# Zero fill of a row buffer moved from GpSimd's queue to SyncE's, with context rows loaded earlier into three buffers

## The chip, the cores and the metric

The kernel runs on one core of a Trainium2 chip, in one launch. The metric is the device time of that launch in microseconds (us): the median over the runs of the program. Five engines of the core take part, each working through its own list of instructions in order: TensorE (PE) multiplies matrices and transposes, VectorE (DVE) and ScalarE (ACT) do elementwise work and reductions, GpSimd (POOL) does the same more slowly and issues indirect transfers, and SyncE (SP) issues most of the plain transfers (DMAs). Engines wait for each other, and for DMAs, on semaphores. All data are float32.

## The reference

A stream `x` of 16 sequences of 128 tokens with 256 channels passes four layers. Each layer is a cross attention to a context `ctx` (16 x 128 x 256), followed by a feed-forward part; both are added to `x` with the weight tanh of a gate. Cut to the first layer, where the change lies:

```python
x = x + tanh(g_xattn[0]) * L0_xattn(ctx, layernorm(x), ctx, Wk, Wq, Wv, Wo)   # 16 heads of 16
x = x + tanh(g_ffn[0])   * L0_ffn(layernorm(x), w_gate, W1, b1, W2, b2)       # 8 experts, the best 2

def L0_xattn(k, q, v, Wk, Wq, Wv, Wo):          # k = v = ctx
    kh, qh, vh = per_head(k, Wk), per_head(q, Wq), per_head(v, Wv)
    attn = softmax(qh kh^T / sqrt(16))
    return concat_heads(attn vh) @ Wo.T

def L0_ffn(x, w_gate, W1, b1, W2, b2):
    gate = softmax(x @ w_gate.T); pick the two largest experts of every token
    return sum over the two of gate_e * (gelu(x @ W1[e] + b1[e]) @ W2[e] + b2[e])
```

The other three layers have the same frame, with other attentions (softmax over queries, a key mask, latents beside the context) and other feed-forward parts (low rank adapters, two more mixtures of experts).

## The kernel before

**Tiling.** The 2048 tokens stand as 16 tiles of 128 tokens, one for each sequence (`b`), and four tiles make a block (`blk`, `BPB` = 4, `NBLK` = 4). For attention layer 0 the class `Fast16` folds the weights of queries and keys into one matrix and those of values and output into another, so keys and values come straight from the context: the keys from its transpose `ctxT` (one tile for each block, loaded through ACT's queue), the values from its rows `ctx_rows` (one tile of 512 KB for each block, loaded through SP's queue).

**Steps of a sequence.** `scores(b)` copies the context rows of `b` into the padded value tile (ACT, L1288), multiplies keys by queries (PE, L1301) and takes the exponential (ACT, L1316). `values(b)` multiplies the exponentials by values and by ones (PE, L1357), takes the reciprocal of the sums into `rs` (DVE, L1368), adds `rs` into a running sum `sum_range` on POOL (L1126; it is looked at once, at the end of the program) and multiplies (DVE, L1370). `output(b)` multiplies by the folded output matrix (PE, L1379) and adds to `x` (DVE, L363). `rs` has two buffers, so the third reciprocal in a row can only start once POOL has read the first.

**Order.** `attend` writes the order of PE, DVE and ACT by hand: it interleaves the steps of 16 sequences with the preparation of the next block (layer norm of `x` with ACT L321 writing `xn`, transposes with PE L344, query projection) and, three steps after a block's last sequence, with the "front" of the mixture of experts of that block (`Moe.front`: a layer norm, the router, positions of the tokens, and the scatter). POOL and SP are not in that hand-written order; a scheduler places their instructions by their dependencies.

**The row buffer.** The mixture of experts sorts tokens by expert: each front writes the normalized rows of its block into a buffer in device memory, `xg` (17,280 rows of 260 numbers, 18 MB), with eight indirect DMAs issued by POOL (L558). Rows that no token takes must be zero, so `xg` is filled with zeros before the first scatter. That is the job of `clear` (L2445 on), a generator that runs ahead of a block's layer norm: for block 1 it makes a tile `zeros` on POOL (L2452) and issues 15 DMAs of 1170 KB on POOL's queue (L2458). For block 2 it issues the first guess of expert weights `w` on SP's queue (L1653), with small bias tiles `b` (L1660, L1667). After the front of block 1 the positions are known, SP reads the plan and fetches rows `xr` and weights, and the expert matmuls (L1701) begin while attention goes on.

**Buffers and queues that the change touches.** `ctx_rows` has two buffers and is loaded by `Fast16.load_rows`: block 0 when the object is made, block `blk + 1` when block `blk` is prepared. `xn` has three buffers, shared by all layer norms. At most eight DMAs of SP and ACT together are in flight: in the built program each waits on a counter for the completion of the one eight before it. POOL's DMAs have eight such counters of their own.

Of the kernel before, what the change touches and what calls it, by code (L numbers as in the profile page):

```python
# [8 lines left out]
F32 = mybir.dt.float32  # L9
# [10 lines left out]
P = 128  # L20
B = 16
S = 128
D = 256
KC = D // P
NBLK = 4
BPB = B // NBLK
TB = BPB * S
# [18 lines left out]
ROWS = NE * REGION + (NE - 1) * P  # L46
# [3 lines left out]
ROW = D + 4  # L50
# [40 lines left out]
def kernel(ctx: ExitStack, tc: tile.TileContext, a: dict, out: bass.AP):  # L91
    nc = tc.nc
# [3 lines left out]
    stat = ctx.enter_context(tc.tile_pool(name="stat", bufs=2))  # L96
    rpool = ctx.enter_context(tc.tile_pool(name="route", bufs=2))
    xtpool = ctx.enter_context(tc.tile_pool(name="xnT", bufs=NBLK))
    class Ring:


        def __init__(self, pool):
            self.pool, self.made = pool, []
# [15 lines left out]
    def load_x(bs):  # L119
        for b in bs:  # L120
            nc.sync.dma_start(out=xs[b], in_=a["x"][b * S:(b + 1) * S, :])
# [9 lines left out]
        out=gates, in_=a["rows"][:, slice(*_ROWS["gates"])].to_broadcast([P, 8])  # L131
# [4 lines left out]
    def col(name, i):  # L136
        lo = _COLS[name][0] + i
        return cols[:, lo:lo + 1]
# [18 lines left out]
    for e in range(NE):  # L157
# [9 lines left out]
        out=tri, in_=ones, compare_op=ALU.is_gt, fill=0.0, base=0,  # L167
# [27 lines left out]
    def tgx(i):  # L195
        return tg[:, i:i + 1]

    def gate_down(pool, i):

        gate = pool.tile([P, 1], F32, tag=f"gate{i}", name="gate", bufs=1)  # L200
        nc.vector.tensor_scalar(gate, tgx(i), DOWN, None, ALU.mult)
        return gate
# [959 lines left out]
    def keys_in(pool):  # L1162
        return lambda: pool.tile([P, KC, TB], F32, tag="kT", name="kT", bufs=2)

    class Fast16:

        def __init__(
            self, layer, pool, kpool, w, ctxT, watch, mask=None, bias=None, others=None  # L1170
        ):

            self.others = others
            self.bias = bias
            self.gate = tgx(1) if layer == 1 else gate_down(pool, layer)
            self.layer, self.pool, self.kpool = layer, pool, kpool
            self.ctxT, self.watch, self.mask = ctxT, watch, mask
            self.w = w

            self.qb = pool.tile([P, KC, 2], F32, tag=f"qb{layer}", name="qb", bufs=1)  # L1180
            if layer == 0:
                nc.vector.memset(self.qb, 0.0)
            else:
                for c in range(KC):
                    nc.vector.tensor_scalar(
                        self.qb[:, c, :], mask2, col(f"l{layer}_bq", c), None, ALU.mult
                    )

            self.vs = []
            for i in range(3):  # L1190
                v = pool.tile([P, H16, 2 * DH16], F32, tag=f"v{layer}{i}", name="v", bufs=1)
                nc.gpsimd.memset(v, 0.0)
                self.vs.append(v)
            self.qM, self.kT, self.es, self.os = {}, {}, {}, {}
            self.rows = {}
            if layer == 0:
                self.kT = dict(enumerate(ctxT))
                self.load_rows(0)

        def load_rows(self, blk):  # L1200

            t = self.pool.tile([P, BPB, D], F32, tag="crows", name="ctx_rows")
            nc.sync.dma_start(
                out=t,
                in_=a["ctx"][blk * TB:(blk + 1) * TB, :].rearrange("(b p) d -> p b d", p=P),
            )
            self.rows[blk] = t

        def prepare(self, blk, before):


            if self.layer == 0 and blk + 1 < NBLK:
                self.load_rows(blk + 1)
            made = [self.queries(blk, before)]
            if blk not in self.kT:
                made.append(self.keys(blk))
            if self.others is not None:

                if blk == 0:
                    made.append(self.keys(1))  # L1220
                for later in (0, 1, 2) if blk == 0 else (3,) if blk == 1 else ():
                    made.append(self.others.keys(later))
            return made
# [1147 lines left out]
    def layers(fast):  # L2371
# [40 lines left out]
        with tc.tile_pool(name="context", bufs=1) as cpool, ExitStack() as for_mid:  # L2412
            ctxT = []

            def load_context(blk):
                t = cpool.tile([P, KC, TB], F32, tag=f"ctxT{blk}", name="ctxT")
                nc.scalar.dma_start(
                    out=t,
                    in_=a["ctxT"][:, blk * TB:(blk + 1) * TB].rearrange("(k p) t -> p k t", p=P),
                )  # L2420
                ctxT.append(t)
# [7 lines left out]
            with tc.tile_pool(name="att0", bufs=2) as pool:  # L2429
                w = attention_weights(0, pool)  # L2430
                if fast:
                    load_x(range(BPB, 2 * BPB))
                load_context(1)
                if fast:
                    nc.sync.dma_start(out=cols, in_=a["cols"])
                    nc.sync.dma_start(out=rows, in_=a["rows"].to_broadcast([P, N_ROWS]))
                    wgs[0] = gate_weights("l0")
                if fast:
                    load_x(range(2 * BPB, B))
                for blk in range(2, NBLK):  # L2440
                    load_context(blk)
                if fast:
                    wgs[2], wgs[3] = gate_weights("l2"), gate_weights("l3")
                moe = Moe(0, wgs[0], first_turn)

                def clear(blk):
                    if blk == 1:


                        n = 9  # L2450
                        zeros = pool.tile([P, 1, 3 * ROW], F32, tag="zeros", name="zeros", bufs=1)
                        nc.gpsimd.tensor_scalar(  # L2452
                            zeros.rearrange("p o (r d) -> p (o r) d", d=ROW),
                            att.kT[0][:, 0:1, 0:ROW].to_broadcast([P, 3, ROW]),
                            0.0, 0.0, ALU.min, ALU.max,
                        )
                        for i in range(0, ROWS, n * P):
                            nc.gpsimd.dma_start(  # L2458
                                out=xg[i:i + n * P, :].rearrange(
                                    "(p r q) d -> p r (q d)", p=P, q=3  # L2460
                                ),
                                in_=zeros.to_broadcast([P, n // 3, 3 * ROW]),
                            )
                    if blk == 2 and fast:
                        moe.guess = {0: 0, 1: 3}
                        for get_some in first0, second0:
                            for lane, e in moe.guess.items():
                                tc.add_manual_dep(
                                    get_some(lanes[lane], e, None).ins, run["aggr"].name,
                                    mybir.DependencyInfo(  # L2470
                                        mybir.DependencyClass.Sync,
                                        mybir.DependencyReason.DATA,
                                    ),
                                    reason="behind the first loads",
                                )
                    if blk == NBLK - 1 and fast:
                        mask.extend(mask_by_keys(cpool, mi))
                    yield 1


                n = full_slots(NBLK // 2) if fast else 0
                turns = {NBLK - 1: cycle((2, 1, 0), NSLOT - n)}
                started = []

                def start(plan):
                    started.append(slots0(moe, n, [plan], lanes, tiles(fpool, bufs0)))

                def early():
                    while not started:
                        yield 1  # L2490
                    yield from started[0]

                if fast:
                    turns[NBLK // 2 - 1] = cycle((0, 1), n)
                    lanes = lane0(fpool, 2)
                else:
                    lanes = []
                behind, plans = routed(moe, turns, start)
                if fast:
                    att = Fast16(0, pool, None, folded(pool, w), ctxT, watch)  # L2500
                    attend([(att, clear, behind)], early(), eager=True, express=2)
                else:
                    general(shifted(pool, 0, w, ctxT), None, behind)
# [5 lines left out]
            with for_slots, tc.tile_pool(name="lanes0", bufs=2) as pool:  # L2509
                lanes = lanes + lane0(pool, LANES - len(lanes))  # L2510
                job = slots0(moe, NSLOT - n, plans[-1:], lanes, tiles(fpool, bufs0))
                for i, _ in enumerate(job):
                    if i == 24:
                        ws = [attention_weights(layer, wpool) for layer in (1, 2)]
                        if not biases:

                            t = stat.tile([P, BPB, ROW], F32, tag="xn", name="bias_rows", bufs=3)
                            nc.sync.dma_start(
                                out=t[:, 0, 0:D],
                                in_=a["l2_b2"][NE:NE + 1].to_broadcast([P, D]),  # L2520
# [60 lines left out]
        with ExitStack() as for_last:  # L2581
# [19 lines left out]
            turns, n = {}, 0  # L2601
# [136 lines left out]
```

## Time and profile before

| what | value |
|---|---|
| time, median of 3 runs | 1607.16 us (1603.55 to 1607.68) |
| profiled execution, its own time | 1651.63 us |
| span of its trace | 1649.8 us |
| PE busy | 1506.4 us (91%) |
| DVE, ACT, POOL busy | 867.0, 639.7, 368.5 us |
| DMA traffic | 173.61 MB, of it 15 transfers of 1170 KB from `zeros` to `xg` |

The profile is of one execution, on the only core. Times in it count from the start of its span. A row of the timeline gives start, duration, engine, line, operation and tiles, the number of instructions merged into it, and in brackets the idle time of the engine ahead of it with what ended that idle time. "SPq" and "POOLq" are the engines' own queues, where issuing a DMA stands. In a table of windows, "DMA share" is the busy share of the 16 DMA engines and "PEclk" the clock that TensorE was granted, as a part of full speed.

### The profile page before, as it was taken

To read this page: it belongs to the slowest core of one execution; us is meant where nothing else is said; L and a number is where in the kernel's file an instruction comes from. 1 tells how busy PE (TensorE), PEld (TensorE's weight loads), DVE (VectorE), ACT (ScalarE), POOL (GpSimd) and SP (SyncE) were. 2 spreads that over 40 slices of the span, in tenths; PEclk is the share of its full clock that TensorE was granted. 3 is DMA by queue.
4 is the path that set the end of the run, shared out by engine and by line. 5 is a ranking of instruction groups with operands and counts; after the bars stand their busy time and mean duration, and the time that the engine had idled before them with its cause. 6 is when DMAs were issued, how large, how long until landed. Compare 5 with 4: busy or idle time off the path is not lost.

```text
span 1649.8 us, 34723 instructions
## 1 busy us (share of the span) xinstructions
PE 1506.4 (91%) x12681; PEld 1178.4 (71%) x12681; DVE 867.0 (53%) x2766; ACT 639.7 (39%) x1538; POOL 368.5 (22%) x485
## 2 busy tenths in 40 slices
PE   5787899999989999999999999999999999888892
PEld 3565789999656567645559999999846665567792
DVE  4666312223289767656346555556734553557564
ACT  4554333335556566452225333334442324123010
POOL 4234211112533112433000111011150002203431
PEclk8897999999999999899999999999999999999896
DMA  9913574524420000111064414310260000024856
GB/s 314 384 60 125 190 244 137 186 85 152 100 33 1 1 14 15 41 40 52 0 220 151 152 42 139 119 33 28 98 122 1 14 5 24 24 85 137 261 175 206
DMA packets 111480, 173.61 MB, mean 105 GB/s; under 512 B 17337, under 2 KB 81406, under 8 KB 111296
## 3 DMA queue, kind: packets, MB, share of 16 engines
q1 hardware_dynamic: 87456, 116.32, 22.4%
q0 software_dynamic: 20304, 49.66, 9.7%
q10 hardware_dynamic: 3536, 5.25, 1.0%
q8 instruction: 107, 1.75, 0.5%
q14 instruction: 77, 0.63, 0.1%
HBM read 274.98 MB, written 48.18 MB: 196 GB/s over the span
## 4 chain that ended last, share of the span: by engine, by line


## 5 line engine op out<-in xcount | busy, mean ns | idle before, releaser
L1878 PEld LDWEIGHTS ps_w<-xT,w 128*128 128x128 f32 x2304 | 264.3, 192 | 2.6 <-issue 0.2
L1878 PE MATMUL ps_w<-xT,w 128*128 128x128 f32 x2304 | 265.0, 275 | 0.0
L878 POOL DMA_INDIRECT yd<-y,to x117 | 118.6, 1014 | 581.2 <-DVE c L841 318.8
L866 PE MATMUL ps_e<-w,hT 128*128 128x256 f32 x848 | 198.5, 380 | 4.1 <-DVE hT L1785 1.9
L866 PEld LDWEIGHTS ps_e<-w,hT 128*128 128x128 f32 x848 | 154.5, 190 | 24.0 <-DVE hT L1785 2.8
L1886 ACT ACTIVATE u<-ps_w,b 128x128 f32<-128x128 f32 x312 | 89.6, 367 | 174.7 <-PE ps_w L1878 165.7
L1889 DVE SCALAR_TENSOR_TENSOR m<-ps_w,b,u 128x128 f32<-128x128 f32 x312 | 87.6, 344 | 108.9 <-PE ps_w L1878 90.7
L1701 PE MATMUL ps_h<-xT,w 128*128 128x128 f32 x1120 | 135.0, 280 | 10.3 <-DMA w<-in_l_w_dram 5.4
L1701 PEld LDWEIGHTS ps_h<-xT,w 128*128 128x128 f32 x1120 | 133.3, 196 | 13.9 <-issue 6.9
L1706 ACT ACTIVATE hT<-ps_h,b 128x128 f32<-128x128 f32 x312 | 88.1, 371 | 134.9 <-issue 81.3
L558 POOL DMA_INDIRECT xg<-xn,xi x96 | 93.5, 974 | 103.9 <-issue 54.6
L1815 PE MATMUL ps_w<-xnT,sw 128*128 128x512 f32 x256 | 113.1, 598 | 0.0
L874 DVE SCALAR_TENSOR_TENSOR y<-ps_e,c,bias 128x256 f32<-128x256 f32 x78 | 37.6, 482 | 133.4 <-PE ps_e L866 132.6
L1126 POOL TENSOR_TENSOR sum_range<-sum_range,rs 128x256 f32<-128x256 f32 x48 | 35.3, 735 | 273.8 <-DVE rs L2295 144.2
L831 DVE COPY xT<-ps_xr 128x256 f32<-128x256 f32 x117 | 48.5, 418 | 84.1 <-PE ps_xr L829 71.1
L1815 PEld LDWEIGHTS ps_w<-xnT,sw 128*128 128x128 f32 x256 | 48.6, 192 | 57.9 <-issue 51.6
L1368 DVE RECIPROCAL rs<-ps_o 128x256 f32<-128x256 f32 x32 | 56.2, 1756 | 59.4 <-PE ps_o L1357 32.3
L1316 ACT ACTIVATE e<-ps_s 128x512 f32<-128x512 f32 x128 | 65.9, 602 | 36.2 <-PE ps_s L1301 33.1
L1357 PE MATMUL ps_o<-e,v 128*32 128x128 f32 x1536 | 58.5, 292 | 15.9 <-issue 4.8
L321 ACT ACTIVATE xn<-x,nmr,rstd 128x256 f32<-128x256 f32 x128 | 67.7, 597 | 13.1 <-DVE nmr L314 9.5
L1357 PEld LDWEIGHTS ps_o<-e,v 128*32 128x32 f32 x1536 | 43.0, 116 | 33.6 <-issue 16.6
L2274 ACT ACTIVATE e<-ps_s 128x512 f32<-128x512 f32 x64 | 33.8, 600 | 80.5 <-PE ps_s L2268 77.1
(280 smaller groups left out, 2566.2 us busy)
## 6 DMA issues: line engine op xcount, KB each, us to landing
w<-in_l_w_dram SPq DMA_DIRECT2D x160, 1024.0 KB
w<-in_l_w_dram SPq DMA_DIRECT2D x39, 512.0 KB
kT<-in_l_wgu_dram SPq DMA_DIRECT2D x39, 512.0 KB
xg<-zeros POOLq DMA_DIRECT2D x15, 1170.0 KB
b<-in_l_b_dram SPq DMA_DIRECT2D x80, 128.0 KB
xr<-xg SPq DMA_DIRECT2D x78, 130.0 KB
kT<-in_l_w_dram SPq DMA_DIRECT2D x39, 256.0 KB
x<-yd POOLq DMA_DIRECT2D x48, 128.0 KB
```

Of the source, the lines that this page charges most:

```text
L321: nc.scalar.activation(xns[:, i, 0:D], src, AF.Identity, bias=nmr[:, i:i + 1], scale=rstd[:, i:i + 1])
L558: self.unordered(nc.gpsimd.indirect_dma_start(out=xg[:, :], in_=xns[:, i, :], in_offset=None, out_offset=bass.IndirectOffsetOnAxis(ap=xi[: ...
L866: nc.tensor.matmul(po, lhsT=hT[:, f, :], rhs=lane(s)["w2"][:, f, :], start=(f == 0), stop=(f == nf - 1),)
L878: self.unordered(nc.gpsimd.indirect_dma_start(out=yd[:, :], in_=y, in_offset=None, out_offset=bass.IndirectOffsetOnAxis(ap=to[:, 0:1], axi ...
L1316: nc.scalar.activation(e, pss[j], AF.Exp)
L1357: nc.tensor.matmul(po[32 * j:32 * (j + 1), i, c, :], lhsT=w if i else v[:, c * HPC + 2 * j + e, :], rhs=es[j][:, 2 * c + e, :], start=(e = ...
L1701: nc.tensor.matmul(ps[:, i, :], lhsT=w["w1"][:, k, f * P:(f + 1) * P], rhs=xT[:, k, :], start=(k == 0), stop=(k == KC - 1),)
L1706: nc.scalar.activation(hT[:, f, :], ps[:, i, :], AF.Gelu, bias=w["b1"][:, f:f + 1])
L1815: nc.tensor.matmul(ps, lhsT=wt[:, k, f * P:(f + 1) * P], rhs=xnT[:, k, :], start=(k == 0), stop=(k == KC - 1),)
L1878: nc.tensor.matmul(ps[:, f, :], lhsT=wt[:, k, s, f * P:(f + 1) * P], rhs=xT[:, k, :], start=(k == 0), stop=(k == KC - 1),)
L1886: nc.scalar.activation(u[:, f, :], pair[0][:, f, :], AF.Identity, bias=w["b1"][:, i:i + 1])
L1889: nc.vector.scalar_tensor_tensor(m1[:, f, :], pair[1][:, f, :], w["b3"][:, i:i + 1], u[:, f, :], ALU.add, ALU.mult,)
```

## The change

The context rows are loaded by a function outside the class, into three buffers. Block 0's rows are loaded on SP's queue ahead of the second four tiles of `x`, block 1's right behind these; block 2's and 3's are loaded when blocks 1 and 2 are prepared. The tile `zeros` is no longer a tile of its own: it takes a buffer of the `xn` ring (three buffers), and it is made from block 1's context rows in place of the transposed context. The 15 zero DMAs are issued by SP: the first six when block 1 is prepared, behind the load of block 2's context rows, and nine more when block 2 is prepared, behind the load of block 3's.

```diff
+    ctx_rows = {}
+    def load_rows(pool, blk):
+        t = pool.tile([P, BPB, D], F32, tag="crows", name="ctx_rows", bufs=3)
+        nc.sync.dma_start(
+            out=t,
+            in_=a["ctx"][blk * TB:(blk + 1) * TB, :].rearrange("(b p) d -> p b d", p=P),
+        )
+        ctx_rows[blk] = t
...
-            self.rows = {}
+            self.rows = ctx_rows
             if layer == 0:
                 self.kT = dict(enumerate(ctxT))
-                self.load_rows(0)
...
-            if self.layer == 0 and blk + 1 < NBLK:
-                self.load_rows(blk + 1)
+            if self.layer == 0 and 1 <= blk < NBLK - 1:
+                load_rows(self.pool, blk + 1)
...
                 if fast:
+                    load_rows(pool, 0)
                     load_x(range(BPB, 2 * BPB))
                 load_context(1)
                 if fast:
+                    load_rows(pool, 1)
                     nc.sync.dma_start(out=cols, in_=a["cols"])
...
+                cleared = []
                 def clear(blk):
+                    n = 9
                     if blk == 1:
-                        n = 9
-                        zeros = pool.tile([P, 1, 3 * ROW], F32, tag="zeros", name="zeros", bufs=1)
+                        zeros = stat.tile([P, BPB, ROW], F32, tag="xn", name="zeros", bufs=3)
+                        zeros = zeros.rearrange("p b d -> p (b d)")[:, None, 0:3 * ROW]
                         nc.gpsimd.tensor_scalar(
                             zeros.rearrange("p o (r d) -> p (o r) d", d=ROW),
+                            ctx_rows[1].rearrange("p b d -> p (b d)")[:, 0:3 * ROW].rearrange(
+                                "p (r d) -> p r d", d=ROW
+                            ) if fast else
                             att.kT[0][:, 0:1, 0:ROW].to_broadcast([P, 3, ROW]),
                             0.0, 0.0, ALU.min, ALU.max,
                         )
-                        for i in range(0, ROWS, n * P):
-                            nc.gpsimd.dma_start(
+                        cleared.append(zeros)
+                    if blk in (1, 2):
+                        at = ROWS * 2 // 5
+                        for i in range(*((0, at) if blk == 1 else (at, ROWS)), n * P):
+                            nc.sync.dma_start(
                                 out=xg[i:i + n * P, :].rearrange(
                                     "(p r q) d -> p r (q d)", p=P, q=3
                                 ),
-                                in_=zeros.to_broadcast([P, n // 3, 3 * ROW]),
+                                in_=cleared[0].to_broadcast([P, n // 3, 3 * ROW]),
                             )
```

`ROWS` is 17,280, `P` 128 and `ROW` 260, so `n * P` is 1152 rows for each DMA and `at` is 6912 rows, six DMAs. In the built program the order of PE, DVE and ACT is the same before and after, instruction by instruction. On SP's queue it becomes: block 0's rows ahead of `x` tiles 4 to 7, block 1's behind them, the other early loads as before, then block 2's rows, six zero DMAs, block 3's rows, nine zero DMAs, then the first guess of expert weights and biases.

More of the change, by code (lines that the diff above doesn't have):

```diff
@@ L1194, in __init__ @@
             self.qM, self.kT, self.es, self.os = {}, {}, {}, {}
-            self.rows = {}
+            self.rows = ctx_rows
             if layer == 0:
                 self.kT = dict(enumerate(ctxT))
-                self.load_rows(0)
[L1200 to L1207, printed above, removed]
         def prepare(self, blk, before):
-            if self.layer == 0 and blk + 1 < NBLK:
-                self.load_rows(blk + 1)
+            if self.layer == 0 and 1 <= blk < NBLK - 1:
+                load_rows(self.pool, blk + 1)
             made = [self.queries(blk, before)]
```

## Prediction

> **What bounds the kernel now.** I read the page first.
>
> ```profile
> span 1649.8 us, 34723 instructions
> PE   5787899999989999999999999999999999888892
> PEclk8897999999999999899999999999999999999896
> DMA  9913574524420000111064414310260000024856
> ```
>
> Each digit is a slice of 41 us. Over the whole span PE is the bound, but not in the first four slices, where the change lies: there PE has 5, 7, 8 and 7 tenths while the 16 DMA engines are full in the first two. So I read the first 160 us as their own stage, by waits and then by timelines of single engines. Two idle stretches of PE stand out. The first, from ACT's timeline:
>
> ```profile
> 20.94 0.78 ACT L1261 ACTIVATE qM<-ps_q,qb,mask 128x512 f32<-128x512 f32 x1 [0.93 <-PE ps_q L975]
> 28.16 0.40 ACT L1288 COPY v<-ctx_rows 128x256 f32<-128x256 f32 x1 [6.44 <-DMA ctx_rows<-in_ctx_dram]
> 28.47 2.05 ACT L1316 ACTIVATE e<-ps_s 128x512 f32<-128x512 f32 x4
> ```
>
> ACT is free at 21.72 and stands until 28.16 for block 0's context rows, which SP issued only at 20.59, its 26th DMA, when zeros (from 19.78) already filled the engines. The exponentials behind it hold PE's score banks. The second, from the timelines of POOL, DVE and PE:
>
> ```profile
> 19.78 6.09 POOL L2458 DMA_DIRECT2D xg<-zeros  x8
> ...
> 50.08 0.72 POOL L2458 DMA_DIRECT2D xg<-zeros  x1 [2.24 <-DMA xg<-zeros]
> 50.70 0.86 POOL L1126 TENSOR_TENSOR sum_range<-sum_range,rs 128x256 f32<-128x256 f32 x1
> ```
>
> ```profile
> 51.59 1.76 DVE L1368 RECIPROCAL rs<-ps_o 128x256 f32<-128x256 f32 x1 [9.79 <-POOL sum_range L1126]
> ```
>
> ```profile
> 42.24 1.06 PE L1357 MATMUL ps_o<-e,ones 128*32 128x128 f32 x32
> ...
> 54.58 2.09 PE L1301 MATMUL ps_s<-qM,ctxT 32*128 32x256 f32 x16 [8.50 <-DVE qM L1256]
> 60.44 1.15 PE L1301 MATMUL ps_s<-qM,ctxT 32*128 32x256 f32 x16
> ```
>
> POOL issues eight zero DMAs, then one more each time an old one lands, until 50.80. The small running sum stands behind them, the third reciprocal stands behind that sum (two buffers), and the queries of block 1 stand behind the reciprocal on DVE: PE waits 8.50 us. Everything after (the other 12 sequences, the fronts, the first expert matmul at 156.62) hangs on this chain, since the order of PE, ACT and DVE is fixed and unchanged. Time taken out here reaches the end, unless something new comes late in its place.
>
> The DMA engines by windows (the last three columns: granted clock, DMA share, GB/s):
>
> ```profile
> 48.00:52.00 4.00, 0.00 (x0) 0.00 (x0) 0.41 (x1) 0.00 (x0) 1.92 (x3) 0.53 1.04 418
> 84.00:88.00 4.00, 4.00 (x74) 2.91 (x76) 3.78 (x10) 1.55 (x5) 0.95 (x2) 1.00 0.62 199
> 88.00:92.00 4.00, 4.00 (x92) 3.06 (x87) 3.60 (x15) 4.00 (x10) 0.17 (x1) 1.00 0.02 4
> ```
>
> They are full from 4 us to about 86 us; then nearly idle. The first scatter follows at 91.83, the positions for it being ready at 90.94.
>
> **The change, part by part.**
>
> *Block 0's rows earlier.* They move from behind SP's 26th DMA (20.59) to the ninth place, where SP stood at 7.14. In flight with the other loads at 230 to 378 GB/s (windows 8 to 16 us) 512 KB need about 2 us, and some of latency: they are there by about 14, before 21.72. The 6.44 us go, but not all is gain: the second half of the first scores is only made at 22.62 to 23.33, so the exponentials start near 23.0 instead of 28.47: **5.5 us**. What is put back by 512 KB (and block 1's 512 KB) are `x` tiles 4 to 15, by 1.5 to 3 us: tiles 4 to 7 are first read at 22.48 and were issued from 7.14 on, the others after 56; hidden. Block 1's `ctxT` on ACT's queue isn't behind them.
>
> *PE's clock there.* The granted clock is 0.55 and 0.50 in the windows from 24 to 32 us. The 16 score matmuls after the stall take 3.53 us, the same 16 at 35.42 take 1.15; the next value matmuls 1.94 against 1.08. Without the stall the clock stays up. Up to 3.2 us of it, but ACT (exponentials and layer norm, back to back) sets the pace there: I take **1.5 us** (0 to 3.2).
>
> *Zero issues off POOL.* POOL loses 15 issues (6.09 us, then seven of 0.72) and 19.9 us of waits between them. What is left for it there, three 1 us scalings of `rows`, comes between 20 and 24, before the first `rs`. The third reciprocal then starts when its matmuls end (42.24 + 1.06 = 43.30) and not at 51.59: **8.2 us**. The clock again: 2.09 against 1.15, 1.94 against 1.08, together 1.9 us; I take **1.5 us**, as DVE's five statistics fill part of it. Sum of gains: 5.5 + 1.5 + 8.2 + 1.5 = **16.7 us**.
>
> *Zero issues on SP.* 15 issues of about 0.4 us (as SP's `ctx_rows` row, 0.38 us) while SP only waits; SP stood from 28.9 to 56.3 with one DMA between. Queued behind them now: block 3's rows, and eight loads of biases and guessed weights. Block 3's rows additionally wait for the fourth value copy (40.03, now about 33.5), and nine zero DMAs stand behind that wait; six zero DMAs, 7.2 MB or 18 to 20 us of transfer, cover it (22 to about 41). Block 3's rows are read at 111. The 4.2 MB of weights, issued at 56 to 71 before, now come behind the fill, until about 88; first read at 156.62 (some 140 after the gain). If that cover were gone, a late microsecond would cost one.
>
> *When the fill ends* is the term that can spoil this, since two things wait for it: POOL (the token column of the second front, then the eight scatters of the first, with the running sums behind these and DVE's reciprocals behind the sums), and ACT's layer norm of the second front, which now takes the buffer of `zeros` (in the built program it waits for all eight hardware DMA counters):
>
> ```profile
> 91.83 1.10 POOL L558 DMA_INDIRECT xg<-xn,xi  x1 [4.93 <-ACT e L1316]
> 107.88 2.07 ACT L321 ACTIVATE xn<-x,nmr,rstd 128x256 f32<-128x256 f32 x4
> ```
>
> Less 16.7 these want the fill done at 75.1 and 91.2. The scatters come first. The fill starts when SP gets there: in front of it are 5.9 MB, against 5.2 MB that had moved by 20 us, so about 22 us. To move until it ends: 18.0 MB of zeros, and 1.5 MB of rows and `x` tiles in between, 19.5 MB. The rate: from 26 to 60 us, when GpSimd's queue had 87% of it, the engines moved 393 GB/s; SP's queue alone with weights (228 to 252 us) 341. This gives 22 + 49.6 = 71.6 and 22 + 57.2 = 79.2. The Trainium skill ("DMA: Bandwidth & Descriptors", Specifications) speaks for caution: it puts a core's limit at the memory at about 358 GB/s, which would give 76.5, 1.4 us too late; the trace has 393 to 418 for long stretches, above that limit, so the measurement decides against it as a ceiling. I still take 360, between the two rows, because SP's queue has never carried zeros in this trace: 76.2, late by 1.1, with the landing's latency 1.5 us. Net **15.2 us**; ends 19 (clock in full, fill early) and 5 (fill at 300 GB/s, end at 87, 12 us late).
>
> The sum is made against the profiled 1651.63: 1636.4. The median of the runs is 44.5 us lower, and nothing shows where; a stretch of 16 us would shrink by 0.4 us in that proportion. So 1607.2 - 15.2 = **1592.0 us**.
>
> **The rivals.**
>
> *The fill comes late and takes a part back* (above): for it, SP's queue at 341; against it, 393 to 418 with zeros. Every microsecond of the end after 75 costs one. At 300 GB/s 1602 us.
>
> *Slower.* The same wait, in one place: POOL stands before the first scatter. It decides from an end of the fill at 75 + 17 = 92, a rate of 19.5 MB / 70 us = 279 GB/s. For it: stretches of 4 us in which SP's queue was busy at 0.75 and moved only 177 (172 us; short packets of the second weights), and the clock loss that a new stall brings along. At 240 GB/s the fill ends at 103 and the time is about 1618 to 1620. Against it: packets of zeros are 3 KB, long ones, and ran at 393.
>
> *No change:* the front's gain is swallowed further on, if the expert stage waits for something with its own pace. For it only 5.4 us of PE waits for weights between 156 and 250 us; against it, those loads are issued from a plan that comes from the same chain, and DMA is nearly idle from 88 to 144. 1607.
>
> *The change doesn't do what it says:* rows land late all the same (x tiles and ACT's loads share the engines). Then 5.5 + 1.5 are not gained, 9.7 are left (the fill is then not late): 1597.5. It needs rows 7 us later than worked out.
>
> **How the numbers follow.** Full gain 0.65 (1586 to 1597), part of it through a late fill or late rows 0.18 (1597 to 1602), no change 0.06, slower 0.11. A measurement here can tell 0.3%, 4.8 us, from no change: faster 0.83, same 0.06, slower 0.11. The range leaves the slower case and part of no change out above, and below 1584 (19 us of gain and 4 us of scatter between runs): 1584 to 1604.
>
> **What would show it.** ACT's first copy of context rows near 21.8 without a wait; no wait of a reciprocal on the running sum near 43; scores of the fifth sequence near 39 in place of 54.58; the clock at or near 1.00 in 24 to 32 and 48 to 56; last zeros landed near 76, first scatter within 2 us of that, first expert matmul near 141. Wrong if the fill ends after 85, if ACT's layer norm of the second front waits on a DMA, or if the first expert matmul comes earlier but the span doesn't shrink with it.

## The result

| | median, us | runs | lowest to highest |
|---|---|---|---|
| before | 1603.58 | 6 | 1598.49 to 1607.68 |
| after | 1592.02 | 6 | 1589.45 to 1593.44 |

The ratio is 0.9923, with a 95% interval of 0.9903 to 0.9943: the changed kernel is 11.6 us faster, and by the interval between 9.1 and 15.6 us (1603.58 times 0.0057 and 0.0097). Forecast were a gain of 15.2 us and a time of 1592.0. The time came out as forecast, the gain did not: the kernel before ran 3.6 us faster in these six runs than the 1607.2 that the forecast started from, and in the profiles the front of the kernel (all that stands before the first expert matmul) gained about 9 us where 15.2 were worked out.

The profiled execution of before on which the prediction rests took 1651.63 us, over 40 us more than its other runs, 43 of them lost behind the first expert matmul; below, the kernel before is read from a second profile of it, of an execution of 1603.36 us, where nothing else is said.

### The profile page after: what moved, and what is told of

It reads as the page before. It is cut to its first block, busy times and chain, and to the rows that moved or that the text cites. A ratio compares the mean times of both kernels' runs of the same rounds, so it can differ in the third digit from the quotient of the medians.

```text
span 1589.2 us, 34722 instructions
## 1 busy us (share of the span) xinstructions
PE 1475.1 (93%) x12681; PEld 1166.8 (73%) x12681; DVE 867.8 (55%) x2766; ACT 639.7 (40%) x1538; POOL 357.8 (23%) x470
## 4 chain that ended last, share of the span: by engine, by line
PE 79%; DVE 10%; DMA 4%; ACT 3%; issue 2%; POOL 1%; SPq 0%; DVEq 0%; POOLq 0%; ACTq 0%
PE ps_w L1879 16%; PE ps_e L866 12%; PE ps_h L1702 8%; PE ps_w L1816 7%; PE ps_qk L2139 5%; PE ps_v L2248 3%; PE ps_o L1358 3%; PE ps_s L1302 2%; PE ps_s L2269 2%; PE ps_q L978 2%; PE ps_g L1927 2%; PE ps_y L2317 2%; PE ps_s L1837 2%; PE ps_y L1380 2%; PE ps_u L1927 2%
## 5 line engine op out<-in xcount | busy, mean ns | idle before, releaser
L866 PEld LDWEIGHTS ps_e<-w,hT 128*128 128x128 f32 x848 | 154.8, 191 | 21.5 <-DVE hT L1786 2.8
L858 ACT ACTIVATE bias<-b,c 128x256 f32<-128x256 f32 x78 | 40.5, 519 | 56.5 <-DVE c L844 21.6
```

Of the source, the lines that this page charges most:

```text
L866: nc.tensor.matmul(po, lhsT=hT[:, f, :], rhs=lane(s)["w2"][:, f, :], start=(f == 0), stop=(f == nf - 1),)
```

## The profile after

The page of the changed kernel, in the rows that the prediction shows of before:

```profile
span 1589.2 us, 34722 instructions
PE   6977989999989999899999999999989999998992
PEclk9987999999999999999999999999999999999996
DMA  9935683534420000111074413411351000033956
```

The first slice of PE went up from 5 to 6 and the second from 7 to 9. The third went down from 8 to 7: something new stands there.

**The first stall is gone.** ACT's timeline of the changed kernel:

```profile
21.69 0.39 ACT L1289 COPY v<-ctx_rows 128x256 f32<-128x256 f32 x1
23.42 2.06 ACT L1317 ACTIVATE e<-ps_s 128x512 f32<-128x512 f32 x4 [1.34 <-PE ps_s L1302]
```

The copy no longer waits for block 0's rows, and the first exponentials come at 23.42 (28.54 before).

**The second stall is gone where it was.** First DVE's and PE's timelines of before, from its second profile, then PE's of the changed kernel:

```profile
51.14 1.76 DVE L1368 RECIPROCAL rs<-ps_o 128x256 f32<-128x256 f32 x1 [8.36 <-POOL sum_range L1126]
...
101.59 1.76 DVE L1368 RECIPROCAL rs<-ps_o 128x256 f32<-128x256 f32 x1 [4.41 <-POOL sum_range L1126]
```

```profile
54.13 2.09 PE L1301 MATMUL ps_s<-qM,ctxT 32*128 32x256 f32 x16 [7.07 <-DVE qM L1256]
...
103.95 1.60 PE L344 MATMUL ps_ln<-ident,xn 128*128 128x128 f32 x8 [4.47 <-DVE oT L1370]
105.48 2.09 PE L1301 MATMUL ps_s<-qM,ctxT 32*128 32x256 f32 x16
...
151.69 5.93 PE L1701 MATMUL ps_h<-xT,w 128*128 128x128 f32 x32 [0.54 <-DVE xT L831]
```

```profile
42.52 1.43 PE L1302 MATMUL ps_s<-qM,ctxT 32*128 32x256 f32 x16 [0.35 <-DVE qM L1257]
...
94.55 1.94 PE L344 MATMUL ps_ln<-ident,xn 128*128 128x128 f32 x8 [7.79 <-DVE oT L1371]
96.42 2.09 PE L1302 MATMUL ps_s<-qM,ctxT 32*128 32x256 f32 x16
...
143.45 6.00 PE L1702 MATMUL ps_h<-xT,w 128*128 128x128 f32 x32 [0.54 <-DVE xT L831]
```

The fifth sequence's scores move from 54.13 to 42.52, 11.6 us. But there is a third stall, which the prediction left out: at about 100 us the same reciprocal waits for the same running sum once more, 4.41 us, here behind the scatters. The changed kernel has it too, and longer. DVE's and POOL's timelines of the changed kernel:

```profile
92.19 1.76 DVE L1369 RECIPROCAL rs<-ps_o 128x256 f32<-128x256 f32 x1 [7.67 <-POOL sum_range L1126]
```

```profile
80.61 0.22 POOL L525 TENSOR_SCALAR xn<-token 128x4 f32<-128x4 f32 x1 [7.73 <-DVE ve L233]
81.44 1.12 POOL L558 DMA_INDIRECT xg<-xn,xi  x1 [0.61 <-issue]
...
90.44 0.96 POOL L558 DMA_INDIRECT xg<-xn,xi  x1 [0.30 <-issue]
91.42 1.54 POOL L1126 TENSOR_TENSOR sum_range<-sum_range,rs 128x256 f32<-128x256 f32 x2
```

POOL stands until 80.61, issues eight scatters, and only then does the sums that DVE waits for. DVE's `ve`, which the first row names, had long been done, and so had the positions: the trace puts their cast (L555, `xi`) at 77.04 to 77.21. In before the first scatter followed 0.89 us behind that cast (89.94 and 90.83), so here it could have come at 78.10. It is 3.3 us late, and the stall grew by 3.3 us, on DVE (7.67 - 4.41) and on PE (7.79 - 4.47). What makes POOL late is the fill: the packets in the trace put the end of the last zeros at 79.96, and SP issues its last load of weights, which has to wait for the last zero DMA, at 80.54. (What stands first on POOL is the token column, which goes into the buffer where the zeros lie; the scatter behind it needs the filled `xg`.)

The end of the fill itself hardly moved. The last packet of zeros ends at 81.96, 81.74 and 80.55 us in the three profiles of before, and at 79.96 and 80.27 in two of the changed kernel. In before nobody stood there, since the positions came only at 89.94; now the front is 12.7 us ahead and runs into it.

So the account of the front, by start times of PE in the two profiles:

| place | before | after | ahead |
|---|---|---|---|
| second sequence's scores | 29.19 | 24.07 | 5.1 |
| fourth sequence | 41.25 | 36.36 | 4.9 |
| fifth | 54.13 | 42.52 | 11.6 |
| sixth | 59.54 | 46.82 | 12.7 |
| twelfth | 93.68 | 80.96 | 12.7 |
| thirteenth, behind the scatters | 105.48 | 96.42 | 9.1 |
| first expert matmul | 151.69 | 143.45 | 8.2 |
| end | 1601.6 | 1589.2 | 12.4 |

Of 12.7 us gained, 3.6 are given back behind the scatters. That the end is ahead by 12.4, more than the first expert matmul, is taken up in the last experiment.

## Experiments

The order of instructions on PE, DVE and ACT is that of before and after in every one of these kernels; what they issue from POOL and SP, and where tiles lie, differs as said.

**Rows early, fill left on POOL.**

```diff
...
-                        for i in range(*((0, at) if blk == 1 else (at, ROWS)), n * P):
-                            nc.sync.dma_start(
+                        for i in range(0, ROWS if blk == 1 else 0, n * P):
+                            nc.gpsimd.dma_start(
...
```

This is against the changed kernel, whose early loads of the rows stay. The zeros lie in a weight tile that is no longer used, and are made from the transposed context as in before.

> Only the context rows move: three buffers, blocks 0 and 1 loaded early; the 15 zero DMAs stay on POOL's queue. (The zeros tile is made from the transposed context, as before, and lies in the place of the dead attention weights.) Theory 'one after the other': ACT's first copy of context rows comes at 21.7 without a wait, but POOL is still held by the zero DMAs until about 50, and the third reciprocal waits for it then as before: the 5 us gained at the first stall are lost at the second, 0 to 1 us in all, 1602 to 1604. Rival 'the two stalls add': 5 us less, about 1598.5.

Measured: 1598.81 us against 1604.38, ratio 0.9965 [0.9951, 0.9979], 5.6 us faster. POOL's, DVE's and PE's timelines:

```profile
16.58 6.10 POOL L2471 DMA_DIRECT2D xg<-zeros  x8 [0.31 <-POOL zeros L2462]
...
45.89 0.73 POOL L2471 DMA_DIRECT2D xg<-zeros  x1 [2.97 <-DMA xg<-zeros]
46.52 0.86 POOL L1126 TENSOR_TENSOR sum_range<-sum_range,rs 128x256 f32<-128x256 f32 x1
```

```profile
47.41 1.76 DVE L1369 RECIPROCAL rs<-ps_o 128x256 f32<-128x256 f32 x1 [9.26 <-POOL sum_range L1126]
```

```profile
50.40 2.09 PE L1302 MATMUL ps_s<-qM,ctxT 32*128 32x256 f32 x16 [7.98 <-DVE qM L1257]
```

The rows come early here too (the copy starts at 22.22 without a wait, 6 us sooner), and all of it is swallowed: the reciprocal waits 9.26 us in place of 8.36, since the sum behind the zeros sets the fifth sequence. That sum is 3.7 us earlier (46.52, before 50.25), and the fifth sequence is 3.7 us earlier with it (50.40, before 54.13). The fill itself began earlier, at 16.58 and not at 19.77: in before the first scaling of `rows` stands ahead of the zero DMAs on POOL and waits for its transfer until 18.88, in this build the scalings come behind them (47.22). So what this gains on PE is that of an earlier fill and not of earlier rows. The time is the one that the rival named (about 1598.5), but not for the rival's reason, and the experiment is no clean one for the rows: what it shows is that PE follows POOL here, not ACT.

**Fill on SP, rows where they were.**

```diff
-                    load_rows(pool, 0)
                     load_x(range(BPB, 2 * BPB))
...
-                    load_rows(pool, 1)
...
             if layer == 0:
                 self.kT = dict(enumerate(ctxT))
+                load_rows(self.pool, 0)
...
-            if self.layer == 0 and 1 <= blk < NBLK - 1:
+            if self.layer == 0 and blk < NBLK - 1:
```

This is against the changed kernel. The zeros have the weight tile of the experiment above, so the fill does not wait for block 1's rows.

> Only the zero fill moves to SP's queue, with three row buffers; the loads of context rows 0 and 1 stand where they stood before, behind the x tiles, and the zeros tile is one of its own made from the transposed context. Theory: the wait of the third reciprocal on POOL goes (8.2 us, and 1.5 us of clock), and the rows of block 0 land a few us earlier too, about 25 instead of 28, since no zeros are in flight in front of them: 11 to 12 us less than before, within 2 us of the whole change. Rival (each part has its own gain): 8 to 9 us, and the rows still 5 us late.

Measured: 1591.40 us, ratio 0.9922 [0.99, 0.9944], 13.0 us faster, as much as the whole change. ACT's and PE's timelines:

```profile
23.91 0.40 ACT L1290 COPY v<-ctx_rows 128x256 f32<-128x256 f32 x1 [3.05 <-DMA ctx_rows<-in_ctx_dram]
```

```profile
42.47 1.43 PE L1303 MATMUL ps_s<-qM,ctxT 32*128 32x256 f32 x16 [0.35 <-DVE qM L1258]
```

With the fill behind them on the same queue, the rows are there at 23.9 though SP issues them nearly as late as before (at 19.74; in before at 20.58, and there at 28.23); PE reaches the fifth sequence at 42.47, as in the changed kernel, where it is 42.52. Once the fill is moved, the early rows add nothing that can be measured: most of the first stall had the same cause as the second, the fill.

**A third buffer for `rs`, nothing else.** The prediction named two buffers as a link of the chain. This takes the link away and leaves the fill on POOL and the rows late.

```diff
-                rs = pool.tile([P, KC, S], F32, tag="rs", name="rs")
+                rs = pool.tile([P, KC, S], F32, tag="rs", name="rs", bufs=3 if self.layer == 0 else 2)
```

> The kernel before with a third buffer for the reciprocals of layer 0; every instruction stands where it stood, fill on POOL included. Theory (the reciprocal waits for a buffer that POOL's running sum holds, and the sum stands behind the zero DMAs on POOL): the wait of 9.8 us at 42 to 51.6 goes, 8 to 10 us less, 1594 to 1596. Rival (the stall is contention of the fill with other transfers): no change.

Measured: 1588.66 us, ratio 0.9893 [0.987, 0.9917], 15.7 us faster: at least as much as the change, with one more buffer and no DMA moved. POOL's and PE's timelines:

```profile
49.10 0.73 POOL L2458 DMA_DIRECT2D xg<-zeros  x1 [2.63 <-DMA xg<-zeros]
49.73 0.86 POOL L1126 TENSOR_TENSOR sum_range<-sum_range,rs 128x256 f32<-128x256 f32 x1
```

```profile
45.81 1.43 PE L1301 MATMUL ps_s<-qM,ctxT 32*128 32x256 f32 x16 [0.28 <-DVE qM L1256]
...
92.35 1.58 PE L344 MATMUL ps_ln<-ident,xn 128*128 128x128 f32 x8
93.87 0.71 PE L1301 MATMUL ps_s<-qM,ctxT 32*128 32x256 f32 x8
```

POOL is as late as before (49.73), and PE is at the fifth sequence 4 us ahead of that sum instead of behind it. The sum itself is short, 0.73 to 0.86 us (DVE's product of the same shape, L1370, takes 0.42); what holds the buffer is the queue in front of it. The gain is larger than expected because the buffer also takes the wait behind the scatters: the layer norm's transposes at 92.35 stand in line with no wait, where before had 4.47 us.

**The changed kernel with four `rs` buffers.** Two are tiles of their own in place of the two before, two lie in weight tiles that are no longer used.

```diff
-                rs = pool.tile([P, KC, S], F32, tag="rs", name="rs")
+                if self.layer == 0:
+                    tag, shape = (
+                        ("rsa", [P, KC, S]), ("rsb", [P, KC, S]),
+                        ("turned", [P, 3, P]), ("w0", [P, 2 * D + 3 * P]),
+                    )[b % 4]
+                    rs = pool.tile(shape, F32, tag=tag, name="rs", bufs=1)
...
```

> The changed kernel with four buffers for the reciprocals of layer 0, in place of two, in dead weight tiles; all orders as in the changed kernel. Theory (in the changed kernel the same queueing comes back behind the eight scatters: reciprocals wait 7.7 and 2.9 us for the running sum, PE 7.8 us at 87 to 94.5 and 5.2 us at 123 to 128.6): these go, 5 to 10 us less than the changed kernel, 1582 to 1587. Rival (PE is held in this stretch by something else as well, as in the kernel before, where it idled there without any wait that the profile shows): 0 to 2 us, 1590 to 1592.

Measured: 1579.77 us, ratio 0.9858 [0.9838, 0.9878] to before: 24.6 us, the best of all, and 12 us faster than the changed kernel. POOL's and DVE's timelines:

```profile
81.38 1.12 POOL L558 DMA_INDIRECT xg<-xn,xi  x1 [0.61 <-ACT e L1317]
...
91.38 1.54 POOL L1126 TENSOR_TENSOR sum_range<-sum_range,rs 128x256 f32<-128x256 f32 x2
```

```profile
82.82 1.75 DVE L1377 RECIPROCAL rs<-ps_o 128x256 f32<-128x256 f32 x1
91.07 1.76 DVE L1377 RECIPROCAL rs<-ps_o 128x256 f32<-128x256 f32 x1 [2.21 <-PE ps_o L1358]
```

POOL's scatters and sums are where they were (81.38 and 91.38; 81.44 and 91.42 without the buffers). DVE's reciprocal no longer waits for them, but for its own matmuls. The thirteenth sequence's scores come at 86.70 in place of 96.42. So the stall of the changed kernel at 87 to 94.5 us is the buffer of `rs`, and the wait for the fill only made it longer.

**Rows early, fill on POOL, a third `rs` buffer.** If the buffer is the link, the queue of the fill should hardly matter once it is gone.

> Context rows early, the zero fill on POOL's queue, and a third buffer for the reciprocals of layer 0. Theory (the zero DMAs on POOL cost only through the reciprocal's buffer): with the buffer the early rows now give their 5 us, so 4 to 6 us less than the kernel before with the third buffer, 1583 to 1585, though the fill never left POOL. Rival (POOL's queue must be free for more than that, or the fill must be on SP): no gain over the third buffer alone, 1588 to 1589.

The edit is the first experiment's, with the third `rs` buffer in a weight tile. Measured: 1581.85 us, ratio 0.9865 [0.9846, 0.9883], 21.5 us faster, and 2 us from the version with the fill on SP and four buffers; the two intervals overlap. One wait of 2.53 us of a reciprocal is left at 47.36. Here the early rows are worth something: 0.9865 against 0.9893 with the buffer alone, 4.5 us of 1603; those two intervals just overlap, but the first expert matmul agrees, 132.74 against 136.76.

**The same fill, from zeros in a tile of their own.** In the changed kernel the zeros lie in a buffer of the layer norm's `xn` ring, which POOL and ACT write again at the second front; the prediction feared a wait there. Here they have a tile of their own and are made from the transposed context.

```diff
-                        zeros = stat.tile([P, BPB, ROW], F32, tag="xn", name="zeros", bufs=3)
-                        zeros = zeros.rearrange("p b d -> p (b d)")[:, None, 0:3 * ROW]
+                        if fast:
+                            zeros = pool.tile([P, 2 * D + 3 * P], F32, tag="w0", name="zeros", bufs=1)
+                            zeros = zeros[:, None, 0:3 * ROW]
...
```

> The changed kernel, but the zeros tile lies in the place of the dead attention weights and is made from the transposed context: no buffer of the layer norms' ring is held, and the fill doesn't wait for context rows. Theory: ACT's layer norm of the second front (85.8 in the changed kernel, fill landed at 80.5) has 5 us to spare, and SP reaches the first zero DMA at 23, after the tile is ready at 19.7 in the changed kernel: no difference, 1590 to 1594. Rival (the ring's wait or the late tile costs): 2 to 5 us less.

Measured: 1593.25 us, ratio to before 0.9935 [0.992, 0.9951], the changed kernel's within the intervals. POOL's token column no longer waits (73.33), but the scatter behind it then waits for the fill itself, until 82.08. The shared buffer costs nothing.

**A longer fill.** Six zero DMAs, 7.2 MB, are issued a second time behind the others.

```diff
-                        for i in range(*((0, at) if blk == 1 else (at, ROWS)), n * P):
+                        for i in (*range(*((0, at) if blk == 1 else (at, ROWS)), n * P), *(range(at, 2 * at, n * P) if blk == 2 else ())):
```

> The changed kernel with six of the 15 zero DMAs issued a second time behind the others: 40% more fill, the same contents. Theory (what waits for the fill's end has no slack any more in the changed kernel): the fill ends 18 us later (7.2 MB at 390 GB/s), near 99, and the time grows by 15 to 18 us, to 1607 to 1610, at or above the kernel before. Rival (slack behind the first scatters): less than 8 us.

Measured: 1598.94 us, ratio to before 0.9975 [0.9966, 0.9985], some 7 us slower than the changed kernel. POOL's, DVE's and PE's timelines:

```profile
77.72 0.73 POOL L1126 TENSOR_TENSOR sum_range<-sum_range,rs 128x256 f32<-128x256 f32 x1 [6.15 <-DVE rs L1369]
81.12 0.74 POOL L1126 TENSOR_TENSOR sum_range<-sum_range,rs 128x256 f32<-128x256 f32 x1 [2.67 <-DVE rs L1369]
...
101.04 1.12 POOL L558 DMA_INDIRECT xg<-xn,xi  x1 [18.86 <-DMA w<-in_l_w_dram]
```

```profile
91.25 1.76 DVE L1369 RECIPROCAL rs<-ps_o 128x256 f32<-128x256 f32 x1 [2.15 <-PE ps_o L1358]
112.12 1.76 DVE L1369 RECIPROCAL rs<-ps_o 128x256 f32<-128x256 f32 x1 [14.69 <-POOL sum_range L1126]
```

```profile
114.49 2.05 PE L1380 MATMUL ps_y<-w_vo,oT 128*128 128x256 f32 x4 [14.42 <-DVE oT L1371]
```

The first scatter follows the fill: 7.2 MB more, 19.6 us later (101.04 - 81.44), which makes 367 GB/s; the engines' mean over the fill of the changed kernel (23 to 80 us) is 366. The last packet of zeros ends at 99.39. The row of POOL names a load of weights, but those go on past the scatter (until 105.4; in the changed kernel until 85.9). That settles that the wait before the first scatter is the fill's. But of 19.6 us only 7 arrive at the end. In this build POOL's program has two of the running sums ahead of the scatters (77.72 and 81.12), where the changed kernel has them behind (91.42). So the reciprocal at 91.25 has its buffer, the layer norm has no wait, and only the next sequence's reciprocal stands, 14.69 us. The forecast "every microsecond of the end after 75 costs one" held in the changed kernel (3.3 us of delay, 3.3 us of stall) and does not hold as a rule: what a late fill costs depends on how many sums stand behind the scatters. With POOL's order changed along, this run cannot say what a late fill would cost in the changed kernel's own order. A shorter fill was not tried.

**Both kernels profiled once more.** The front is ahead by 8.2 us, the end by 12.4. Is the rest a gain in the expert stage?

> The kernel before once more, for a second profile, since its first profiled execution took 1651.63 us, 47 us over the median of its runs. Theory: the two stalls at the front are the same (rows near 28, reciprocal on the running sum until near 51), the 47 us are elsewhere, and the span is near 1603. In the stretch behind the first scatters either PE again idles with no wait shown (as at 97 to 103 in the first profile), or a reciprocal waits for the running sum behind the scatters, as in the changed kernel.

> The kernel before, unchanged, profiled once more. Open is why the changed kernel is 8.2 us ahead at the first expert matmul (151.69 against 143.45) and 12.4 us at the end: from that matmul to the end the kernel before took 1449.9 us and the changed one 1445.8. Theory A, scatter of executions: this stretch is 1446 to 1453 in any execution of either kernel, and here differs from 1449.9 by 2 us or so. Theory B, the change also shortens the expert stage: 1449 to 1451 here. The front must repeat under both: fifth sequence's scores at 53 to 55, first expert matmul at 151 to 152.5.

> The changed kernel, profiled once more, for the same question. Theory A, scatter: from the first expert matmul to the end anything from 1446 to 1450. Theory B, a property of the change: 1445 to 1447. The front repeats under both: fifth sequence's scores at 42 to 43, first scatter at 81 to 82, reciprocal behind the running sums waiting 7 to 8 us, first expert matmul at 143 to 144.

| profile | time | fifth sequence | thirteenth | first expert matmul | from there to the end |
|---|---|---|---|---|---|
| before, second profile | 1603.36 | 54.13 | 105.48 | 151.69 | 1449.9 |
| before, third profile | 1601.43 | 54.17 | 106.68 | 153.16 | 1446.4 |
| after, first profile | 1591.03 | 42.52 | 96.42 | 143.45 | 1445.8 |
| after, second profile | 1596.60 | 42.82 | 96.74 | 143.76 | 1451.0 |

In these four the front repeats within 1.5 us. The rest does not: from the first expert matmul to the end before took 1449.9 and 1446.4 us and after 1445.8 and 1451.0. (The profile that the prediction used lies outside: 156.62, and 1493.2 from there on; no run shows why.) The other kernels lie in the same band, 1446.2 (four `rs` buffers), 1447.4 (fill on SP), 1447.6 (own zeros, and rows with a third buffer), 1449.5 (longer fill), 1450.9 (rows early) and 1452.3 (third `rs` buffer alone). So the 4 us are no property of the change that these profiles show; they are no more than the scatter of the expert stage between executions. The gain that these profiles show for the change is that of the front, 7.9 to 9.7 us (151.69 or 153.16 less 143.45 or 143.76), at the lower edge of the interval of the runs, 9.1 to 15.6. Whether the 2 us and more up to the 11.6 of the medians are scatter too stays open.

## Why the prediction was right, and where not

The time was right, 1592.02 for 1592.0, and a match as close as that is luck: two errors of 3.6 us cancel. The forecast took 15.2 from 1607.2, the median of three runs; over six runs the kernel before came out at 1603.58, and the gain at 11.6. (The range of 1584 to 1604 takes in the kernel before as well.) What was right in substance is the chain that holds the front up: zero DMAs on POOL, the sum behind them, the buffer of `rs`, the reciprocal. The fill moved alone and the buffer alone both show it. The single steps were not all right.

*Block 0's rows earlier*, 5.5 us: near in size (5.1 at the second sequence and 4.9 at the fourth in the table, 5.0 and 3.9 against the profile that the prediction used; 3.9 and 3.4 between the third profile of before and the second of after), wrong in worth. With the fill on POOL the next stall swallows it; with the fill on SP most of it comes by itself. It is worth something only where the `rs` wait is gone too.

*PE's clock there*, 1.5 us (0 to 3.2): nothing. The step took for granted that the stall had brought the clock down and that without it the clock stays up. Windows of the changed kernel (the last three columns are the granted clock, the DMA share and GB/s):

```profile
24.00:28.00 4.00, 3.93 (x28) 2.72 (x32) 1.52 (x9) 3.26 (x10) 0.00 (x0) 0.64 0.92 303
28.00:32.00 4.00, 4.00 (x68) 3.35 (x64) 0.75 (x1) 3.10 (x7) 0.00 (x0) 0.50 1.03 403
...
48.00:52.00 4.00, 4.00 (x88) 3.07 (x92) 3.79 (x10) 3.62 (x8) 0.97 (x2) 1.00 1.02 388
52.00:56.00 4.00, 4.00 (x80) 3.42 (x84) 3.62 (x8) 3.97 (x12) 0.83 (x2) 1.00 1.03 386
...
88.00:92.00 4.00, 0.00 (x0) 0.00 (x0) 0.00 (x0) 0.48 (x1) 3.38 (x4) 0.75 0.55 198
```

The clock is at 0.64 and 0.50 from 24 to 32 us with the stall gone, and the 16 score matmuls at 24.07 take 3.54 us there, as the 3.53 of before. By the clock records of the traces the low stretch is shorter (25.1 to 32.0 us, where the prediction's profile of before has 24.4 to 34.6), but PE's lead does not grow over it, 5.1 at the second sequence and 4.9 at the fourth. The two rows from 48 on belong to the step below. The last row is the new place of the old stall: PE has no instruction from 88 to 92 us, while DVE and ACT stand as well and POOL issues scatters.

*Zero issues off POOL*, 8.2 and 1.5 us: the mechanism is right, shown by the fill moved alone and, from the other side, by the buffer alone. The size, 9.7, came out as 6.7 at the fifth sequence (11.6 - 4.9) and 7.8 from the sixth on (12.7 - 4.9). Here the clock did come: it is 1.00 from 48 to 56 us, where before had 0.53 and 0.50 (0.79 and 0.50 in the second profile), the fifth sequence's scores take 1.43 us in place of 2.09, and the lead grows by 1.1 from the fifth to the sixth. (The two differences that the prediction adds up to 1.9 make 1.8.) How it divides from the step before is loose: the reciprocal's wait is 9.79, 8.36 and 9.64 us in three profiles of before, and the fifth sequence comes at 54.58, 54.13 and 54.17 in all three, since POOL sets it. Only the sum of both steps means something: 16.7 forecast, 12.7 measured (13.6 against the profile that the prediction used). Of the 4.0 missing, 2.1 are missing by the fourth sequence (7.0 forecast for the rows and the first clock term, 4.9 measured) and 1.9 between there and the sixth.

*Zero issues on SP*, hidden: nothing in the runs contradicts it. PE's waits for the experts' first weights are 6.7 us in the changed kernel and 6.9 in before, from 140 us on.

*When the fill ends*: 76.2 forecast, 79.96 measured (last packet of zeros; POOL goes on at 80.61). Up to its last hundredth the fill came as forecast, by two errors that cancel: its first packet moves at 26.1 and not at 22, and from 26 to 60 us the engines move 390 GB/s and not the 360 taken; so 99% of the zeros have landed at 75.2. (For the rate the prediction took 418 GB/s for a long stretch too, which was one window of 4 us, and packets of 3 KB, which on POOL's queue were of 6,240 bytes.) The last hundredth takes until 79.96. The prediction let the guessed weights come behind the fill; they are issued behind it, but in the trace their packets begin at 74.0, and 1.4 MB of them, with 0.25 MB of biases, move before the last zeros. That they hold the last zeros up is likely and not shown, since no run leaves them out. The mean over all, 366 GB/s from 23 to 80 us, lies between the two rows of the prediction, 341 and 393, and above the 358 that it quotes from the Trainium skill ("DMA: Bandwidth & Descriptors", Specifications).

*Late by 1.5*, net 15.2: the mechanism held, the size did not. The scatter is late by 3.3 us against the positions and each of them costs one, as the prediction charged it; 3.6 us of the lead are given back in place of 1.5. What the prediction did not see is that before has a stall of the reciprocal behind its scatters already (4.41 us in its second profile). The change neither makes nor removes that part; it is what a third buffer takes away.

The sum of the front, corrected: 5.1 - 0.2 + 7.8 - 3.6 is 9.1 at the thirteenth sequence, and 8.2 at the first expert matmul, in place of 15.2. *The fill comes late and takes a part back* was the rival at 0.18 and is what happened in the front, though the time lies in the range of the full gain, because before was faster than taken. The *slower* rival, fill end at 92, did not come: SP's queue would have had to stay below 279 GB/s. Its price is open, since the longer fill, which ended at 99.4 and was still 4 us faster than before, had POOL's order changed with it. *Rows land late all the same* fell with the copy at 21.69. *No change* fell with the interval.

Of what the prediction said would show it, the first copy (21.69 for 21.8) came as written; the fifth sequence (42.52 for 39), the first expert matmul (143.45 for 141) and the scatter (81.44 for about 77) came 2 to 5 us late; the clock came from 48 to 56 us and did not from 24 to 32. ACT's layer norm of the second front did not wait for a DMA.

## What to carry to other kernels

When an engine waits for another that "issues DMAs", look first at what ties the two together: here a bookkeeping sum that nobody needed soon held two small buffers, and one more buffer was worth 15.7 us where moving 15 DMAs to another queue was worth 11.6. A stall that is removed at one place can come back where the same tie is loaded again, as it did here behind the scatters, so follow the tie through the whole stage before adding up a gain. And where a gain is read from one profiled execution, profile the same kernel a second time: a stage of 1450 us scattered by 5 us between two executions of the changed kernel, near half of the gain in question.

## What the runs showed of the hardware that was not expected

- The 16 score matmuls of the second sequence take 3.53 or 3.54 us in every profile, where the fourth sequence's take 1.15: in the changed kernel at 24.07 behind a wait of 0.67 us, with the fill alone moved at 24.86 behind 2.39, in before at 29.19 behind 5.69. The long stall ahead of them is thus not what makes them slow. Taken singly, they differ in two things: in the changed kernel PE waits four times, 2.1 us in all, for the exponentials of the sequence before, and a single matmul takes 629 ns at the median, against 374 at 36.4 us. The clock row shows 0.50 to 0.69 from 24 to 32 us in the runs read for it, which fits, but in the second profile of before it shows 1.00 beside the same 629 ns. (The first clock record of that profile stands only at 36.6 us, those of the others looked at between 20 and 22, so its 1.00 need not be a measurement.) What makes the single one slow stays open.
- Which queue issued the fill made no difference to the pace of the DMA engines. From 26 to 60 us they moved 390 GB/s with the zeros on SP's queue (389 in the second profile), and 393, 392 and 387 with them on GpSimd's. The packets differed all the same: the zeros went in packets of 3,120 bytes from SP's queue (128 ns each at the median) and of 6,240 bytes from GpSimd's (239 ns).
